# Moving the weighted sums and denominator sums to the end of TensorE's step, and the widening of the maxima behind the step's exponentials

## The chip, the cores and the metric

The kernel runs on one core of a Trainium2 chip. The metric is device time in microseconds (us) of one execution; the times given are medians of several runs. A core has five engines, each of which works through its own list of instructions in the order written: TensorE (matrix products, PE in the profile; its weight loads are PEld), VectorE (DVE), ScalarE (ACT), GpSimd (POOL) and SyncE (SP), which here issues the DMA transfers. [...]

## The reference, cut to what matters

The input is 8 sequences of 1024 rows of 512 numbers. Three stages follow each other, each added to its input:

```
x = x + 0.5 * ffn(layernorm(x))
x = x + attention(layernorm(x))
x = x + 0.5 * ffn(layernorm(x))

ffn(l):        q_l = round(l / scale of the row), q_r = round(rhs / scale of the column), both int8
               (q_l @ q_r) * scale of the row * scale of the column
attention(y):  q, k, v = y Wq', y Wk', y Wv'      16 heads of 32
               q, k = layernorm within each head, with gain and offset
               att = softmax(causal(q k' / sqrt(512)))
               (att v) Wo' + bo
```

What the change concerns is the attention: for each head, the scores, the exponentials of the scores less a maximum per row, their sums weighted by v, and the sums of the exponentials (the denominators).

## The kernel before, in words

**Units.** A unit is one sequence and one group of four heads: 8 x 4 = 32 units (`units`, class `Unit`). Each unit goes through a projection of its rows to q, k and v (`project`, `take`, `squares`, `logs`, `divide`, `turn`), a first pass over the scores to get each row's maximum (`m_*`), and a second pass for the exponentials and sums (`e_*`). The three are done in three successive iterations k: while unit k does its second pass, unit k+1 does its first pass and unit k+2 is projected. The feed-forward stages are cut into blocks of 128 rows (`First` before the attention, `Last` after it) and spread over the same iterations.

**Steps.** An iteration has 20 steps. Nothing is left to a scheduler: every piece of work is entered in a table by `at(k, s, rank, function)`, for iteration k, step s (which may exceed 19 and then falls into the next iteration) and a rank. The last loop of the kernel walks the steps in order, and in a step the entries by rank, and calls them. Each call writes its instructions at the end of the lists of the engines that it uses. So the rank is the order within a step on every engine's list at once, DMA issues on SP included. Ranks are named in one line:

```
    FILL, SUM, MISC, REST, BULK, ADD = range(6)
```

**FILL** (`fill`, L709) is the core of a step: causal masks for the first pass (`m_masks`, L480: bfloat16 matmuls with full 128 x 128 weights), the score matmuls of first and second pass in turn (L496, L566: weights of 32 rows, so that four heads share the array), then VectorE's maximum (`m_max`, L514, L523) and ScalarE's exponential (`e_exp`, L589). Where a block touches the diagonal, GpSimd zeroes the masked half of the exponentials (L593). The last unit has no first pass and does its steps in pairs (`fill_both`).

**SUM** holds `e_sum` (L621), the weighted sums: float32 matmuls with weights of 128 rows and 32 columns, one block of columns for each of the four heads, so a third form of the array. `e_sum(i)` is due two steps after the first half of the exponentials that it reads, at step 2i+2: every even step from 2 to 20. It also holds `e_den` (L639), the sums of the denominators, with weights of ones in the same form, at steps 10 and 22, and ScalarE's copy of the result (L647), which `e_fold` at the next step sends off by four DMAs. `e_den` reads what `e_add` (L609, GpSimd; in the last unit also VectorE) has added up from all blocks.

**MISC** holds transposes and the products of the feed-forward: `flip` (L299, at even steps; it transposes the rounded input that ScalarE wrote at L294 and copies the result at L301), `product` (L306), `spread` (L348), `turn` (L456), and `m_both` (L530), in which VectorE merges two sets of maxima at step 17. **REST** holds work of the other engines: `take`, `e_out`, `e_fold`, loads and stores. **BULK** holds the large matmuls with full weights: `Unit.project` (L402, half a block of rows in each step) and `Last.project` (L368, L370). **ADD** holds `e_add`, and at the end of the first pass `m_wide`, `m_turn` and `m_shift`: ScalarE widens the 32 maxima of a partition to 1024 numbers (L535), TensorE transposes them (L543), VectorE adds them to q (L553), so that the second pass's scores come out less the maximum.

**Buffers.** Each of the accumulators of scores, `p_s` and `p_t`, has one buffer, so the scores of a step wait for the maximum and the exponential of the step before. `ps_x` is one buffer in turn for `flip`, `product`, `spread`, `turn` and `e_den`. Exponentials have four buffers of each of two kinds.

Of the kernel before, what the change touches and what calls it, by code (L numbers as in the profile page):

```python
# [55 lines left out]
def macaron_kernel(  # L56
# [198 lines left out]
    def places(pool, **bufs):  # L255
        return {tag: (pool, tag, n) for tag, n in bufs.items()}
# [482 lines left out]
    def at(k, s, rank, fn, *args):  # L739
        plan[k * STEPS + s].append((rank, len(plan[k * STEPS + s]), fn, args))  # L740

    bufs = places(work, y=3, qn=2, qT=2, f=3, xin=2, x1r=1, x2=1)
    FILL, SUM, MISC, REST, BULK, ADD = range(6)
    def last(f, k, s0):
        at(k, s0, BULK, f.project, 0)
        at(k, s0 + 1, BULK, f.project, 1)
        for s, rank, fn in (
            (-1, REST, f.load),
            (2, REST, f.begin),
            (3, REST, f.root),  # L750
            (4, REST, f.scale),
            (5, REST, f.whole),
            (6, MISC, f.flip),
            (7, MISC, f.product),
            (8, REST, f.add),
            (9, REST, f.store),
        ):
            at(k, s0 + s, rank, fn)

    for k in range(-1, NU + 1):  # L760
        eu = units[k] if 0 <= k < NU else None
        mu = units[k + 1] if 0 <= k + 1 < NU else None
        pu = units[k + 2] if 0 <= k + 2 < NU else None
        for s in range(STEPS):
            m = mu if s < 2 * len(MTILES) else None
            if k == NU - 1:
                if s % 2 == 0:
                    at(k, s, FILL, fill_both, eu, s // 2)
            elif eu is not None or m is not None:
                at(k, s, FILL, fill, eu, m, s)  # L770
        if eu is not None:
            for i in range(len(ETILES)):
                at(k, 2 * i + 2, SUM, eu.e_sum, i)
                for pr in range(2):
                    eng = nc.vector if k == NU - 1 and pr else nc.gpsimd
                    at(k, 2 * i + pr + 1, ADD, eu.e_add, i, pr, eng)
            for hf, s in ((0, 7), (1, 21)):
                at(k, s, REST, eu.e_out, hf)
            for hf, s in ((0, 7 if k == NU - 1 else 10), (1, 22)):
                at(k, s, SUM, eu.e_den, hf)  # L780
                at(k, s + 1, REST, eu.e_fold, hf)
                at(k, s + 3, REST, eu.e_rec, hf)
                at(k, s + 5, REST, eu.e_wide, hf)
                at(k, (15 if k == NU - 1 else 20, 31)[hf], REST, eu.e_mult, hf)
        if mu is not None:
            at(k, 17, MISC, mu.m_both)
            at(k, 17, ADD, mu.m_wide)
            at(k, 18, ADD, mu.m_turn)
            at(k, 18, ADD, mu.m_shift, 0)
            at(k, 18, ADD, mu.m_shift, 1)  # L790
        if pu is not None:
            for t in range(NT):
                s = 2 * t if t < 4 else 2 * t + 2
                at(k, s, BULK, pu.project, t, 0)
                at(k, s + 1, BULK, pu.project, t, 1)
                at(k, s + 2, REST, pu.take, t)
            for j, s in enumerate((4, 8, 14, 18)):
                at(k, s + 1, REST, pu.squares, j)
                at(k, s + 2, REST, pu.logs, j)
                at(k, s + 3, REST, pu.divide, j)  # L800
            for j, s in enumerate((11, 13, 21, 23)):
                at(k, s, MISC, pu.turn, j)

        b, j = divmod(k + 6, 4)
        if 0 < b < B and (b, j) != (1, 0):
            for n in range(2):
                f = First(b, 2 * j + n, ps_x, bufs)
                for s, rank, fn in (
                    (2, REST, f.load),
                    (4, REST, f.begin),  # L810
                    (5, REST, f.root),
                    (6, REST, f.scale),
                    (7, REST, f.whole),
                    (8, MISC, f.flip),
                    (9, MISC, f.product),
                    (10, REST, f.add),
                    (11, REST, f.store),
                    (12, REST, f.root2),
                    (13, REST, f.norm2),
                    (16, MISC, f.spread),  # L820
                ):
                    at(k, s + 10 * n, rank, fn)

        b, j = divmod(k, 4)
        b -= 1
        if 0 <= b < B - 1:
            for n in range(2):
                last(Last(b, 2 * j + n, ps_x, bufs), k, (10 * n + 8) if k < NU - 1 else (6 * n + 4))
# [49 lines left out]
```

## Time and profile before

| what | value |
|---|---|
| median of 3 runs | 2504.11 us (2503.69 to 2505.66) |
| profiled execution, its own time | 2508.39 us |
| its span, first to last instruction | 2506.7 us |
| TensorE, VectorE, GpSimd, ScalarE busy | 95%, 71%, 67%, 49% of the span |
| mean granted TensorE clock | 0.988 |
| score matmuls busy, first pass L496, second pass L566 | 656.6 and 663.2 us |
| q, k, v projections busy, L402 | 773.7 us |
| weighted sums busy, L621 | 340.7 us |
| additions of exponentials busy on GpSimd, L609 | 1109.7 us |
| widening of the maxima, L535, 32 times | 1.06 us each |

From about 170 us to about 2320 us the iterations follow one another with little difference, some 67 us each; before that lies the preparation of weights and the first sequence, after it the last unit and the last blocks of the output. A busy time of TensorE is a sum over modelled ends of overlapping matmuls, so a lost tenth of a microsecond is more safely read from the starts of successive groups than from idle time.

### The profile page before, as it was taken

What the parts mean: (1) busy time and instruction counts of PE and PEld (TensorE: products, weight loads), DVE (VectorE), ACT (ScalarE), POOL (GpSimd) and SP (SyncE); (2) the same over time, 40 slices, a digit from 0 to 9 for tenths busy, and PEclk for the clock granted to TensorE, in tenths of its full rate; (3) what the DMA queues carried; (4) which work ended last, traced back from release to release, by engine and by line L of the source; (5) the groups of instructions that cost most, each with busy time, mean ns of one, the idle gap of its engine ahead of it and who ended that gap; (6) DMA issues with size and microseconds to landing.
All of it is one profiled execution on the core that took longest, in us unless ns stands there. A gap on an engine that the chain in (4) does not pass through costs nothing.

```text
span 2506.7 us, 40820 instructions
## 1 busy us (share of the span) xinstructions
PE 2392.0 (95%) x15448; PEld 1099.6 (44%) x15448; DVE 1778.8 (71%) x3053; ACT 1237.1 (49%) x2409; POOL 1681.9 (67%) x1790
## 2 busy tenths in 40 slices
PE   3999999999999999999999999999999999999785
PEld 1544444444444444444444444444444444444332
DVE  9566777777777777777777777777777776666664
ACT  2335555555554555555555555555555555545441
POOL 3227777776777776677777667777767776666672
PEclk9899999999999999999999999999999999999997
DMA  4000000111110111111011111111111100000011
GB/s 143 30 18 22 27 26 27 31 41 38 33 42 31 43 35 35 39 35 43 31 43 35 35 39 35 43 32 35 44 35 39 35 28 25 27 27 27 26 43 59
DMA packets 79303, 92.86 MB, mean 37 GB/s; under 512 B 30977, under 2 KB 37121, under 8 KB 79106
## 3 DMA queue, kind: packets, MB, share of 16 engines
q1 hardware_dynamic: 79106, 90.26, 11.8%
q8 instruction: 121, 1.98, 0.3%
q14 instruction: 76, 0.62, 0.1%
HBM read 55.60 MB, written 34.08 MB: 36 GB/s over the span
## 4 chain that ended last, share of the span: by engine, by line
PE 76%; DVE 12%; POOL 7%; issue 4%; SPq 1%; ACT 1%; DMA 1%; DVEq 0%; POOLq 0%; ACTq 0%
PE p_qkv L402 22%; PE p_s L496 17%; PE p_o L621 9%; PE p_w_b L370 8%; PE p_t L566 6%; POOL pt L609 4%; DVE nm L523 3%; PE p_f_b L306 2%; PE p_d L639 2%; PE p_s L480 2%; PE p_f_a L306 2%; PE p_h L456 2%; POOL f_b L313 2%; DVE oT L674 1%; PE p_m L543 1%
## 5 line engine op out<-in xcount | busy, mean ns | idle before, releaser
L609 POOL TENSOR_TENSOR pt<-pt,pt 128x768 f32<-128x768 f32 (+1 forms) x630 | 1109.7, 1764 | 127.0 <-ACT pt L589 108.5
L589 ACT ACTIVATE pt<-p_t 128x1024 f32<-128x1024 f32 (+1 forms) x640 | 599.4, 938 | 982.4 <-PE p_t L566 908.4
L523 DVE TENSOR_REDUCE nm<-p_s 128x2 f32<-128x1024 f32 (+2 forms) x640 | 632.9, 1006 | 525.8 <-PE p_t L566 409.6
L402 PE MATMUL p_qkv<-wall,yT_a 128*128 128x384 f32 x2048 | 773.7, 501 | 0.2 <-ACT v L421 0.2
L496 PE MATMUL p_s<-qk 32*128 32x512 f32 (+3 forms) x3072 | 656.6, 524 | 14.1 <-DVE nm L523 12.4
L566 PE MATMUL p_t<-qk 32*128 32x512 f32 (+3 forms) x3072 | 663.2, 526 | 2.0 <-ACT pt L589 2.0
L402 PEld LDWEIGHTS p_qkv<-wall,yT_a 128*128 128x128 f32 x2048 | 354.7, 191 | 287.3 <-issue 136.6
L593 POOL TENSOR_SCALAR_AFFINE_SELECT pt<-pt 128x256 f32<-128x256 f32 x512 | 227.6, 457 | 215.6 <-ACT pt L589 214.2
L621 PE MATMUL p_o<-pt,v 128*32 128x512 f32 (+3 forms) x3072 | 340.7, 497 | 11.8 <-POOL pt L593 11.6
L496 PEld LDWEIGHTS p_s<-qk 32*128 32x128 f32 x3072 | 227.5, 185 | 198.0 <-DVE nm L523 65.6
L566 PEld LDWEIGHTS p_t<-qk 32*128 32x128 f32 x3072 | 238.7, 183 | 52.2 <-ACT pt L589 23.5
L370 PE MATMUL p_w_b<-wo,oT 128*128 128x512 f32 x512 | 244.3, 600 | 0.0
L621 PEld LDWEIGHTS p_o<-pt,v 128*32 128x32 f32 x3072 | 75.1, 108 | 247.8 <-issue 159.0
L313 POOL TENSOR_TENSOR f_a<-f_a,xin_a 128x512 f32<-128x512 f32 x64 | 90.9, 1420 | 84.2 <-DVE f_a L310 84.2
L480 PEld LDWEIGHTS <-ident_bf 128*128 128x128 bf16 x1024 | 83.5, 98 | 135.9 <-issue 81.2
L462 ACT ACTIVATE qk<-p_h,qk_b,qk_g 128x256 f32<-128x256 f32 x256 | 130.1, 563 | 11.9 <-PE p_h L456 11.9
L370 PEld LDWEIGHTS p_w_b<-wo,oT 128*128 128x128 f32 x512 | 97.6, 192 | 78.0 <-issue 69.1
L480 PE MATMUL p_s<-causal_bf,ident_bf 128*128 128x128 bf16 x1024 | 110.2, 220 | 8.6 <-DVE nm L523 5.8
L514 DVE TENSOR_REDUCE nm<-p_s 128x4 f32<-128x1024 f32 x64 | 77.6, 1212 | 47.2 <-PE p_t L566 42.6
L417 ACT ACTIVATE sq<-p_qkv 128x256 f32<-128x256 f32 x256 | 99.1, 387 | 21.7 <-PE p_qkv L402 15.1
L420 ACT COPY c<-p_qkv 128x256 f32<-128x256 f32 x256 | 96.8, 378 | 4.3 <-PE p_h L456 4.3
L313 POOL TENSOR_TENSOR f_b<-f_b,x_b 128x512 f32<-128x512 f32 x64 | 89.9, 1405 | 8.9 <-DVE f_b L310 8.9
(108 smaller groups left out, 2474.0 us busy)
## 6 DMA issues: line engine op xcount, KB each, us to landing
xin_a<-in_x_dram SPq DMA_DIRECT2D x64, 256.0 KB, 2.8
x1d_a<-f_a SPq DMA_DIRECT2D x64, 256.0 KB, 2.2
rb<-rdr SPq DMA_DIRECT2D x256, 64.0 KB, 2.0
x1r_b<-x1d_a SPq DMA_DIRECT2D x64, 256.0 KB, 2.9
out_dram<-f_b SPq DMA_DIRECT2D x64, 256.0 KB, 2.1
dsq<-dsb SPq DMA_DIRECT2D x256, 2.0 KB, 1.7
rT<-in_rhsT_dram SPq DMA_DIRECT2D x4, 256.0 KB, 3.6
wall<-in_wqT_dram SPq DMA_DIRECT2D x4, 256.0 KB, 5.8
```

The lines of the kernel that those rows point to most:

```text
L313: nc.gpsimd.tensor_tensor(self.f, self.f, self.src, ALU.add)
L370: nc.tensor.matmul(self.p_w, oT[self.b, g, hf][:, o : o + P], wo[:, g, :], start=False, stop=(g == NG - 1),)
L402: nc.tensor.matmul(self.p[:, : 3 * P], yT[self.b, t][:, kc, :], wall[:, kc, self.g].rearrange("p a f -> p (a f)"), start=(kc == 0), stop=( ...
L462: nc.scalar.activation(self.qk[:, a, 2 * j * P : (2 * j + 2) * P], p_h[:, a].rearrange("p t i -> p (t i)"), AF.Identity, scale=qk_g[:, a : ...
L480: nc.tensor.matmul(self.pm[:, hh, c0 + n - P : c0 + n], ident_bf, causal_bf, start=not self.pm_begun, stop=False, skip_group_check=True,)
L496: nc.tensor.matmul(self.pm[:, hh, c0 : c0 + n], self.rows(0, h, it * P, P), self.rows(1, h, ch * HALF, n), start=not self.pm_begun and sub ...
L523: nc.vector.tensor_reduce(self.nm[:, ch, it, hs], self.pm[:, :, c0 : c0 + n], AX.X, ALU.max, negate=True)
L566: nc.tensor.matmul(self.pes[pr][:, hh, c0 : c0 + n], self.rows(1, h, jt * P, P), self.rows(0, h, hf * HALF + o, n), start=True, stop=True, ...
L589: nc.scalar.activation(pt[:, :, :cols], self.pes[pr][:, :, :cols], AF.Exp, scale=scale)
L593: nc.gpsimd.affine_select(out=pt[:, :, c0 : c0 + P], in_=pt[:, :, c0 : c0 + P], compare_op=ALU.is_ge, fill=0.0, base=0, pattern=[[0, 2], [ ...
L609: eng.tensor_tensor(acc[:, :, o : o + n], acc[:, :, o : o + n], pt[:, :, c0 : c0 + n], ALU.add)
L621: nc.tensor.matmul(self.p_o[h * HD : (h + 1) * HD, o : o + n], self.v[:, jt, h * HD : (h + 1) * HD], self.pt[i, h // 2][:, h % 2, c0 : c0 ...
```

## The change

Two edits in the table of steps; no instruction is added or removed. The rank SUM goes from second place to fifth: within a step, `e_sum` and `e_den` now come behind MISC, REST and BULK, and ahead of ADD only. And `m_wide` goes from the end of step 17 (rank ADD) to step 18 at rank MISC, where it stands right behind that step's FILL, ahead of `flip`'s and `take`'s copies on ScalarE; `m_turn`, which needs it, stays at the end of step 18.

```
-    FILL, SUM, MISC, REST, BULK, ADD = range(6)
+    FILL, MISC, REST, BULK, SUM, ADD = range(6)
...
         if mu is not None:
             at(k, 17, MISC, mu.m_both)
-            at(k, 17, ADD, mu.m_wide)
+            at(k, 18, MISC, mu.m_wide)
             at(k, 18, ADD, mu.m_turn)
             at(k, 18, ADD, mu.m_shift, 0)
             at(k, 18, ADD, mu.m_shift, 1)
```

More of the change, by code (lines that the diff above doesn't have):

```diff
@@ L742, in macaron_kernel @@
     bufs = places(work, y=3, qn=2, qT=2, f=3, xin=2, x1r=1, x2=1)
-    FILL, SUM, MISC, REST, BULK, ADD = range(6)
+    FILL, MISC, REST, BULK, SUM, ADD = range(6)
     def last(f, k, s0):
@@ L786, in macaron_kernel @@
             at(k, 17, MISC, mu.m_both)
-            at(k, 17, ADD, mu.m_wide)
+            at(k, 18, MISC, mu.m_wide)
             at(k, 18, ADD, mu.m_turn)
```

## The prediction

> **What bounds the kernel now.** I read the busy row first, then TensorE's waits between 180 and 2320 us (before lie the weights, after it the last unit), then TensorE's instructions in order of time in one unit, then those of GpSimd and ScalarE in the same microseconds.
>
> ```profile
> PE 2392.0 (95%) x15448; PEld 1099.6 (44%) x15448; DVE 1778.8 (71%) x3053; ACT 1237.1 (49%) x2409; POOL 1681.9 (67%) x1790
> ```
>
> TensorE sets the time. Its waits:
>
> ```profile
> PE p_o L621 <- POOL pt L593: 10.3, 26, 0.7
> PE p_s L496 <- DVE nm L523: 6.6, 26, 0.6
> ```
>
> That looks like 10 us to win. But idle time counts from a modelled end, so I measure from start to start. TensorE, steps 18 and 19 of unit 16 (columns: start, length, then the group):
>
> ```profile
> 1224.94 0.70 PE L566 MATMUL p_t<-qk 32*128 32x256 f32 x4
> 1225.57 0.84 PE L621 MATMUL p_o<-pt,v 128*32 128x384 f32 x4
> 1226.77 1.06 PE L621 MATMUL p_o<-pt,v 128*32 128x384 f32 x12 [0.36 <-POOL pt L593]
> 1227.76 0.40 PE L299 MATMUL p_t_a<-ident_bf,qn_a 128*128 128x128 bf16 x4
> 1228.00 0.38 PE L368 MATMUL p_w_b<-bo,ones_bf 128*128 128x512 bf16 x1
> 1228.21 1.88 PE L370 MATMUL p_w_b<-wo,oT 128*128 128x512 f32 x4
> 1229.93 1.04 PE L543 MATMUL p_m<-ident,nmw 128*128 128x128 f32 x8
> ```
>
> The weighted sum `e_sum(8)` takes 1227.76 - 1225.57 = 2.19 us. The same sixteen matmuls unwaited:
>
> ```profile
> 2335.59 1.07 PE L621 MATMUL p_o<-pt,v 128*32 128x384 f32 x16
> 2336.59 0.40 PE L299 MATMUL p_t_b<-ident_bf,qn_b 128*128 128x128 bf16 x4
> ```
>
> 1.00 us, so 1.19 is lost where the wait says 0.36. Who is late? GpSimd, then ScalarE:
>
> ```profile
> 1222.47 1.55 POOL L313 TENSOR_TENSOR f_b<-f_b,x_b 128x512 f32<-128x512 f32 x1
> 1223.98 2.35 POOL L609 TENSOR_TENSOR pt<-pt,pt 128x1024 f32<-128x1024 f32 x1
> 1226.28 0.80 POOL L593 TENSOR_SCALAR_AFFINE_SELECT pt<-pt 128x256 f32<-128x256 f32 x2
> ```
>
> ```profile
> 1224.62 0.62 ACT L294 ACTIVATE qn_a<-y_a 128x512 bf16<-128x512 f32 x1
> 1226.40 1.06 ACT L535 ACTIVATE nmw<-nm 128x1024 f32<-128x1024 f32 x1 [1.15 <-DVE nm L530]
> 1227.36 0.58 ACT L589 ACTIVATE pt<-p_t 128x512 f32<-128x512 f32 x1
> ```
>
> The masking (L593) of step 17's exponentials stands behind an addition of the feed-forward and one of denominators. ScalarE has waited 1.15 us for the maxima, and step 18's exponential stands behind that; nobody on TensorE waits for it.
>
> **What the Trainium skill says.** TensorEngine Tiling (Array Packing), Key Properties: a change of tiling mode drains TensorE. The trace agrees: 384-column matmuls with full weights start 0.322 us apart, but 0.414 pass from the last to the first score matmul (1203.803 to 1204.217), so 0.09 is the drain. Perfetto Trace Analysis, Tensor Engine Instruction: the end of a matmul is estimated, not observed; 0.36 against 1.19 shows what that hides. SBUF — State Buffer, SBUF: two separate sides: VectorE with two inputs in SBUF and GpSimd lock each other out. L530 is 0.18 us at its shortest and 1.55 at the median, and here ends at 1226.36, with the addition on GpSimd (1226.33). That is why the maxima are late.
>
> **Part 1, sums to the end: what it removes.** I compared each run of matmuls of one kind with the shortest of the same shapes and neighbours. Between 200 and 2310 us only these exceed it noticeably.
> - `e_sum(8)`, step 18: 1.17 us in units 4 to 25, 0.59 in units 0 to 3, 0.27 in 26 to 29, 1.16 in 30. In front of it now come the transposes `flip` (0.23) and `Last.project` (1228.00 to 1229.93, plus a drain: 2.03). That is more than the 1.19 needed; in units 0 to 3 only `flip` is there, and 0.33 of 0.59 is won. 22 x 1.17 + 4 x 0.33 + 4 x 0.27 + 1.16 = 29.3 us.
> - `e_sum(9)`, step 20, units 0 to 3: 1.29 each. A projection (1.49) comes in front: 5.2 us.
> - Scores waiting for VectorE's maxima at steps 13 and 14: 0.14 + 0.27 in 22 units, 8.9 us. The same work lies between the same scores, so I count nothing; they are the upside.
> Removed: 34.5 us.
>
> **What it adds.** Modes in order before: scores (32x128), sum (128x32), full weights, next scores: three changes. After: scores, full, sum, scores: three again. But where the next step opens with the causal masks, which have full weights, they followed the full matmuls without a change, and now follow the sum.
>
> ```profile
> 1220.88 1.46 PE L402 MATMUL p_qkv<-wall,yT_a 128*128 128x384 f32 x4
> 1222.17 0.28 PE L480 MATMUL p_s<-causal_bf,ident_bf 128*128 128x128 bf16 x2
> 1222.37 0.70 PE L496 MATMUL p_s<-qk 32*128 32x512 f32 x2
> ```
>
> 1.29 us for the projection into masks, where into scores it takes 1.385 (the median of those behind a transpose): one drain more. The change from full weights to a sum appears once without a wait:
>
> ```profile
> 2433.35 0.39 PE L368 MATMUL p_w_b<-bo,ones_bf 128*128 128x512 bf16 x1
> 2433.58 1.88 PE L370 MATMUL p_w_b<-wo,oT 128*128 128x512 f32 x4
> 2435.39 0.64 PE L621 MATMUL p_o<-pt,v 128*32 128x256 f32 x8
> ```
>
> 2.04 us against 1.94 (2316.42 to 2318.36) into more full weights: 0.093 to the nanosecond. Four masks behind a sum take 0.327 (2331.37 to 2331.70), behind full weights 0.316. So about 0.10 each. Masks open odd steps 1, 3, 5, 9, 17, all behind a sum: 31 units x 5, less six with nothing moved in between, 149 x 0.10 = 14.9 us. In step 18 the transposes `m_turn` (0.97 us, 1229.93 to 1230.90) followed full weights and now follow the sum: a drain of 0.093 plus weights that load uncovered, 0.057 by the first float32 transpose after a change (0.165, later ones 0.109): 31 x 0.15 = 4.7 us. I take 0.10 and 0.15; the ends are 0.08 to 0.15 and 0.13 to 0.25, that is 16 to 30 us together.
>
> **Other things moved, costed at nothing.** `flip` loses its cover: it now follows the scores. Its input was done 0.27 to 0.59 us before the sum began (here 1225.24 against 1225.57), so no wait; the margin is thin in 102 flips. `spread`'s input has over 5 us, buffers of the projections 2.7 and more. `e_den` ends a step: its copy L647 (0.59) is ready 1.28 us after the last matmuls' start (tail: 2441.30 to 2442.58), and `turn` wants the bank after 0.54 + 1.07 = 1.61. Queued behind the copy on ScalarE is the next exponential, which needs later scores anyhow. SP's four `e_fold` DMAs come about 1.5 us later; behind them stand the store of `x1d`, the next loads and the reciprocal's DMA, due two steps (7 us) on. GpSimd's `e_add(4)` waits for `e_sum(3)`, some 2 us later; it sat idle 3.0 us before and 3.1 after (start 1190.9).
>
> **Part 2, the widening.** L535 (1.06) starts behind step 18's exponential, which moves from 1227.36 to about 1225.7; L535 itself stays near 1226.4, held by L530, and ends 1227.5. `m_turn` needs it near 1228.8. Behind it stand `flip`'s copy (to 1228.1) and three of `take` (1.06), wanted in steps 19 and 20. Gain and loss: nothing; uncovered it would cost up to 1 us in 31 units.
>
> **Last unit.** Steps have no projections to move past, but a `flip` at step 10 that waits for ScalarE (0.34) now waits in front of the sum (+1.1), and some eight changes of mode (0.8 in all); `flip` at step 22 no longer waits for `e_den`'s copy (-1.7), yet that sum comes 2.4 us later, with over 3 to spare before its reciprocal at 2450.24 (DMAs issued until 2444.96, 1.7 to land). I take +2, between -2 and +4.
>
> **Sum.** -34.5 + 14.9 + 4.7 + 2 = -12.9 us. The profiled execution took 2508.4 us (span 2506.7), so 2495.5; the median 2504.1 stands 4.3 below it and gives 2491.2. Ends: -34.5 + 16 - 2 = -20.5 (2483.6) and -34.5 + 30 + 4 = -0.5 (2503.6).
>
> **Rivals.**
> - The listed wait is the true one: 10.3 us plus little, less 20 and 2: +11, 2515. Against it, start to start shows 1.19. Chance 0.04.
> - GpSimd stays late: as TensorE arrives sooner, half the wait comes back at `e_sum(9)` or in the next unit: -17 + 22 = +5, 2509. Against it, GpSimd idles 2 to 3 us at several places in each unit. 0.12.
> - Slower: `flip` waits. Its margin is a median 0.33 to 0.59. If its input comes later by the margin plus d, TensorE loses 102 x d; from d = 0.17 the result is over 2509, at 0.25 it is 2517. For it: the thin margin. Against: nothing ahead of L294 on ScalarE or VectorE moves. 0.08.
> - The upside: VectorE's 8.9 us go too: 2482. For it, masks at step 9 start 0.1 later; against, the lag begins at step 11. 0.10.
> - My sum, 0.66, mostly 2484 to 2504.
>
> A measurement can't tell 0.2% (5.0 us) from no change. Below 2499.1: most of my sum (0.6), the upside, little else: 0.72. Within: 0.16. Above 2509.1: 0.12. To hold eight in ten I take 2481 to 2507.
>
> **What would show it.** Step 18: score, flip, project, then one group of sixteen L621 of 1.0 us without a wait, `m_turn` of about 1.03 right behind. Odd masked steps longer by 0.10. The wait L621 for L593 near zero. Wrong if waits appear at L299 for L294, or if changes of mode cost over 0.19 each (34.5 / 180).

## The result, and the profile after

The changed kernel takes 2493.72 us (median of 5 runs, 2492.61 to 2494.24) against 2504.11 us before; the ratio is 0.9961 with a 95% interval of 0.9946 to 0.9975, so between 6 and 14 us faster. Predicted were 2491.2 us and -12.9 us. The profiled execution took 2492.61 us with a span of 2490.9; the one of before had 2506.7, and was itself some 4 us slower than its median.

The first part of the page hardly changes: TensorE is as full as it was.

```profile
PE 2377.0 (95%) x15326; PEld 1082.3 (43%) x15448; DVE 1780.6 (71%) x3053; ACT 1222.0 (49%) x2409; POOL 1678.6 (67%) x1790
```

Some 122 matmul records are missing from this trace, so that of the sums is taken from starts, not from busy time. TensorE's waits between 180 and 2310 us:

```profile
PE p_s L496 <- DVE nm L523: 6.6, 26, 0.6
PE p_w_b L370 <- issue: 1.3, 8, 0.2
PE p_m L543 <- ACT nmw L535: 0.9, 4, 0.2
PE p_s L480 <- DVE nm L523: 0.9, 1, 0.9
```

The wait of the weighted sums L621 for the masking L593 is gone (10.3 us before); that of the scores for VectorE's maxima is the same to a tenth; a new one, of 0.9 us in all, is that of `m_turn` for the widened maxima. The second line stands where the record of the matmul in front (L368) is among those missing. TensorE in step 18 of unit 16, the step shown of before:

```profile
1214.46 0.70 PE L566 MATMUL p_t<-qk 32*128 32x256 f32 x4
1215.09 0.40 PE L299 MATMUL p_t_a<-ident_bf,qn_a 128*128 128x128 bf16 x4
1215.54 1.88 PE L370 MATMUL p_w_b<-wo,oT 128*128 128x512 f32 x4
1217.35 1.07 PE L621 MATMUL p_o<-pt,v 128*32 128x384 f32 x16
1218.35 1.09 PE L543 MATMUL p_m<-ident,nmw 128*128 128x128 f32 x8
1219.38 0.70 PE L566 MATMUL p_t<-qk 32*128 32x256 f32 x4
```

The sum is one group of sixteen and takes 1.00 us (1217.35 to 1218.35) where it took 2.19. The transposes behind it take 1.03 us (1218.35 to 1219.38) where they took 0.97. From the first score of step 18 to the first of step 19 pass 4.92 us; before it was 5.96. GpSimd and ScalarE in the same stretch:

```profile
1213.37 2.35 POOL L609 TENSOR_TENSOR pt<-pt,pt 128x1024 f32<-128x1024 f32 x1
1215.67 0.79 POOL L593 TENSOR_SCALAR_AFFINE_SELECT pt<-pt 128x256 f32<-128x256 f32 x2
```

```profile
1215.27 0.60 ACT L589 ACTIVATE pt<-p_t 128x512 f32<-128x512 f32 x1 [0.51 <-PE p_t L566]
1215.78 1.05 ACT L535 ACTIVATE nmw<-nm 128x1024 f32<-128x1024 f32 x1
```

GpSimd is nearly as late: its masking ends at 1216.46, 1.37 us after TensorE went on from the scores of step 18 (1215.09); before it was 1.51 (1227.08 against 1225.57). Only, TensorE now has other work until 1217.35. ScalarE no longer sits idle for the maxima.

What did it cost? Step 16 ends like this, with the masks of step 17 behind the sum:

```profile
1209.29 1.46 PE L402 MATMUL p_qkv<-wall,yT_a 128*128 128x384 f32 x4
1210.68 1.07 PE L621 MATMUL p_o<-pt,v 128*32 128x512 f32 x8
1211.68 0.28 PE L480 MATMUL p_s<-causal_bf,ident_bf 128*128 128x128 bf16 x2
1211.89 0.70 PE L496 MATMUL p_s<-qk 32*128 32x512 f32 x2
```

The projection takes 1.39 us into the sum, where it took 1.29 into the masks. I read that 0.09 to 0.10 us as the added change of the array's mode; e3 and e9 below test it.

A unit's length is best measured from one unit's first `m_turn` (L543) to the next one's, in the instructions in order of time. The table gives it for the units with the same make-up, worked out so from each profile. It also shows that units differ more than the "some 67 us each" given for the kernel before: from 66 to 74 us.

| kernel | units 1 to 3 | units 5 to 25 | units 27 to 29 | first L543 to last, us |
|---|---|---|---|---|
| before | 66.02 | 73.57 | 69.49 | 2223.5 |
| the change | 65.03 | 73.08 | 69.91 | 2208.7 |
| e1, sums alone | 65.06 | 73.09 | 69.91 | 2206.4 |
| e2, widening alone | 66.02 | 73.57 | 69.49 | 2223.3 |
| e3, sums of steps 2, 4, 8, 16 | 66.22 | 73.88 | 69.80 | 2230.6 |
| e4, sum of step 18 (20 in 0 to 3) | 64.84 | 72.41 | 69.22 | 2188.5 |
| e9, e4 with `m_turn` behind | 64.83 | 72.55 | 69.37 | 2191.5 |

So the change is a gain of 0.49 us in each of 21 units and of 0.99 in three, and a loss of 0.42 in three. Of the 15.8 us between the two spans, 14.8 lie between the first and the last L543. The 2.0 us ahead of it touch nothing that was changed; that stretch varies between 158.5 and 161.6 us over all but one of the profiles of this study. The last stretch is 1.0 us longer.

### The profile page after: what moved, and what is told of

It is laid out like the page before. It is cut to its first block, busy times and chain, and to the rows that moved or that the text cites. A ratio compares the mean times of both kernels' runs of the same rounds, so it can differ in the third digit from the quotient of the medians.

```text
span 2490.9 us, 40698 instructions
## 1 busy us (share of the span) xinstructions
PE 2377.0 (95%) x15326; PEld 1082.3 (43%) x15448; DVE 1780.6 (71%) x3053; ACT 1222.0 (49%) x2409; POOL 1678.6 (67%) x1790
## 4 chain that ended last, share of the span: by engine, by line
PE 83%; DVE 12%; issue 3%; ACT 1%; SPq 1%; POOL 1%; DMA 0%; DVEq 0%; POOLq 0%; ACTq 0%
PE p_qkv L402 24%; PE p_s L496 18%; PE p_o L621 10%; PE p_w_b L370 9%; PE p_t L566 7%; DVE nm L523 3%; PE p_s L480 3%; PE p_d L639 2%; PE p_f_b L306 2%; PE p_h L456 2%; PE p_f_a L306 2%; PE p_y_a L348 1%; PE p_m L543 1%; DVE oT L674 1%; DVE amax_b L281 1%
## 5 line engine op out<-in xcount | busy, mean ns | idle before, releaser
L593 POOL TENSOR_SCALAR_AFFINE_SELECT pt<-pt 128x256 f32<-128x256 f32 x512 | 226.0, 453 | 199.3 <-ACT pt L589 194.1
L621 PE MATMUL p_o<-pt,v 128*32 128x512 f32 (+3 forms) x3072 | 315.8, 496 | 0.0
L621 PEld LDWEIGHTS p_o<-pt,v 128*32 128x32 f32 x3072 | 72.2, 109 | 209.0 <-issue 160.2
L480 PEld LDWEIGHTS <-ident_bf 128*128 128x128 bf16 x1024 | 71.5, 98 | 171.4 <-issue 134.4
```

The source lines that it names most:

```text
L480: nc.tensor.matmul(self.pm[:, hh, c0 + n - P : c0 + n], ident_bf, causal_bf, start=not self.pm_begun, stop=False, skip_group_check=True,)
L593: nc.gpsimd.affine_select(out=pt[:, :, c0 : c0 + P], in_=pt[:, :, c0 : c0 + P], compare_op=ALU.is_ge, fill=0.0, base=0, pattern=[[0, 2], [ ...
L621: nc.tensor.matmul(self.p_o[h * HD : (h + 1) * HD, o : o + n], self.v[:, jt, h * HD : (h + 1) * HD], self.pt[i, h // 2][:, h % 2, c0 : c0 ...
```

## The experiments

All are timed in turn with the kernel before on the same chip; its medians there were 2505.7 to 2507.4 us, so each is read by its ratio.

**The two halves apart (e1, e2).** e1 is the change without this edit, e2 is this edit alone:

```
-            at(k, 17, ADD, mu.m_wide)
+            at(k, 18, MISC, mu.m_wide)
```

> Theory (all of the gain comes from the sums' new rank): about -10 us, the same as the whole change, 2493 to 2495; m_turn still finds its input, since the widening was held by VectorE's merge of the maxima in both places. Rival (the widening's place matters, because step 18's exponential no longer stands behind it): at least 3 us of the gain are missing here, and units 0 to 3 wait at step 20 again.

> Theory (nothing on TensorE waited for the exponential behind the widening): no change, 2502 to 2506. Rival (the exponential of step 18 comes 1.6 us earlier and GpSimd's masking with it): 3 us or more faster.

e1 took 2494.39 us (ratio 0.9958, 0.9945 to 0.997), e2 2505.82 us (1.0003, 0.9995 to 1.0011). The order of the sums carries everything. The widening's place is worth nothing, in either order of the sums: units of 5 to 25 differ by 0.01 us. In units 1 to 3 of the change it moves time from one step to the next: `m_turn` waits for it, and step 18 takes 3.42 us where e1 has 3.14, but step 19 takes 1.80 where e1 has 2.10.

**Where the order only costs (e3).** The sums go to the end in four steps in which they had not waited, and with them the sum of the denominators that falls into step 2.

```
+    FILL, SUM, MISC, REST, BULK, TURN, LATE, ADD = range(8)
+    late = k < NU - 1 and i in (0, 1, 3, 7)
+    at(k, 2 * i + 2, LATE if late else SUM, eu.e_sum, i)
+    at(k, s, LATE if k < NU - 1 and hf else SUM, eu.e_den, hf)
```

> The sums go to the end only in steps 2, 4, 8 and 16 of iterations 0 to 30, where the next step opens with masks and no sum waited. Theory (each such sum adds one change of the array's mode, 0.10 us): 122 x 0.10 = +12 us, about 2516. Rival (a change of mode is hidden, or the order within a step is free): 2504 within 2 us.

It took 2513.49 us, 1.0033 (1.0021 to 1.0046): slower by 5 to 12 us where I expected 12. A unit grows by 0.31 us and not by 4 x 0.10. The trace shows why: the sum of step 18, measured from its first start to the next group's, takes 2.04 to 2.08 us here and 2.16 to 2.20 before (iterations 4 to 25). In one unit:

```profile
1230.87 0.84 PE L621 MATMUL p_o<-pt,v 128*32 128x384 f32 x4
1231.92 1.06 PE L621 MATMUL p_o<-pt,v 128*32 128x384 f32 x12 [0.22 <-POOL pt L593]
1232.91 0.40 PE L299 MATMUL p_t_a<-ident_bf,qn_a 128*128 128x128 bf16 x4
```

The tenth that step 16 loses is taken from the wait of step 18, since GpSimd's masking does not come later with it. The three other steps show it in full: 0.093 us for the projection's end into the sum, and 0.01 for the masks behind the sum (0.327 against 0.316 for four). In the change itself, where step 18 no longer waits, nothing absorbs the fourth.

**Only where the sum waits (e4).** In step 18 the transposes of the maxima also come ahead of the sum, from iteration 4 on, so that they keep their neighbours of the same mode (LATE and TURN are the ranks of e3).

```
+    late = k < NU - 1 and (i == 8 or i == 9 and k < 4)
+    at(k, 2 * i + 2, LATE if late else SUM, eu.e_sum, i)
+    at(k, 18, MISC, mu.m_wide)
+    at(k, 18, TURN if k >= 4 else ADD, mu.m_turn)
```

> The sum goes to the end only in step 18, and in step 20 of iterations 0 to 3; in step 18 the transposes of the maxima come ahead of it from iteration 4 on, so that they follow full weights. Theory (only there did the sum wait, and without the masked steps nearly no change of mode is added): -34.5 + 1 = -33 us, 2469 to 2474, faster than both kernels. Rival (as TensorE comes sooner, GpSimd is late elsewhere): half of it, 2485 or more, with waits of L621 for L593 at another step.

It took 2473.32 us, 0.9875 (0.986 to 0.989), and again 2473.13 (0.9869, 0.9853 to 0.9886). That is some 32 us faster than before and some 20 faster than the change. Its TensorE, one unit:

```profile
1207.50 0.40 PE L299 MATMUL p_t_a<-ident_bf,qn_a 128*128 128x128 bf16 x4
1207.95 1.88 PE L370 MATMUL p_w_b<-wo,oT 128*128 128x512 f32 x4
1209.67 1.04 PE L543 MATMUL p_m<-ident,nmw 128*128 128x128 f32 x8
1210.64 1.07 PE L621 MATMUL p_o<-pt,v 128*32 128x384 f32 x16
1211.64 0.70 PE L566 MATMUL p_t<-qk 32*128 32x256 f32 x4
```

The projection takes 1.72 us into the transposes, and these 0.97 into the sum. A unit is 1.16 us shorter than before: the whole wait of 1.17. The change has 0.67 us more in a unit than this kernel: five masked steps and the transposes, for which the prediction had 5 x 0.10 + 0.15 = 0.65.

**The price of the transposes' place (e9).** e4 without its last line.

> The kernel with only step 18's sum moved, but with the transposes of the maxima left behind the sum, as in the change. Theory (full weights to sum to full weights is one change of mode more, 0.093, and the first transpose's weights load uncovered, 0.06): the unit is 0.15 us longer than with the transposes ahead, 27 units x 0.15 = +4 us, about 2477.5. Rival (the price is in the masked steps alone): no difference, 2473.

> The same kernel as e4_step18, beside e9_turn_behind on the same chip, so that the two are compared there: 2470 to 2476.

2473.46 us (2471.85 to 2475.68) beside 2473.13 (2470.37 to 2474.98): the medians do not tell them apart. The profiles do: a unit is 72.55 us against 72.41, 0.14 where 0.15 was expected, and the difference lies in step 18 (4.92 us against 4.77). But the stretch behind the last L543 is 4.0 us shorter than in the second profile of e4 (120.8 against 124.8), which hides it in the total. The granted clock differs there: 0.91 in that stretch of e9, 0.88 in that of e4. I take the price as shown by the units, and its share of the time as not measured.

**Was GpSimd's order the cause? (e5)** The sums stay early; one addition goes behind the masking that it held up.

```
-    at(k, 2 * i + pr + 1, ADD, eu.e_add, i, pr, eng)
+    late = k < NU - 1 and (i, pr) == (7, 1)
+    at(k, 2 * i + pr + 1 + late, ADD, eu.e_add, i, pr, eng)
```

> The sums stay early; on GpSimd alone one addition of denominators (block 7, second pair of heads) goes from the end of step 16 to the end of step 17, behind the masking of step 17's exponentials. Theory (the sum of step 18 waits because that masking stands behind this addition): the wait of step 18 goes, about -27 us, 2476 to 2481; a little may come back at step 20. Rival (GpSimd is late by its whole load, not by the order): the wait moves to step 20 in all units, gain under 12 us.

It took 2491.15 us, 0.9937 (0.9923 to 0.9951): -16 us, not -27. In units 5 to 25 the reading holds: they shrink to 72.48 us, by 1.09. Step 18 gains 1.16, and step 20 loses 0.07. But units 1 to 3 grow from 66.0 to 68.2, and 27 to 29 from 69.5 to 70.3. In units 27 to 29 the sum of step 20 waits 1.06 us. Units 1 to 3 gain 0.59 in step 18 and lose 2.03 in step 19 by a new wait of TensorE, the first line below. What is late there stands in the rows after it, of GpSimd and VectorE around one step 18:

```profile
PE p_s L480 <- DVE qk L553: 9.0, 4, 2.3
```

```profile
290.31 5.48 POOL L609 TENSOR_TENSOR pt<-pt,pt 128x1024 f32<-128x1024 f32 x3
290.40 2.32 DVE L445 TENSOR_TENSOR hh<-hh,hss 128x16 f32<-128x16 f32 x1
```

Three additions now follow one another, and an operation of VectorE on 16 columns, 0.18 us at its median and 1.76 at most in the kernel before, takes 2.32. It ends with the first addition (292.71 and 292.68); the next one, L447, takes 1.73 and ends with the second. The shift of q stands behind them, and the next unit's masks wait for that. A further 0.7 to 0.8 us goes in step 20 of these units. Behind the new wait the granted clock was 0.50 for 3.4 us (from 229.2 and 297.5 us on, and twice more), while the kernel before had 1.00 throughout these units; whether the clock or GpSimd costs these 0.7 us no run tells. So the delay in step 18 belongs to GpSimd's order, and a new order puts it somewhere else unless the steps there have room.

**What flip lost (e6, e7).** ScalarE writes the input of each flip (L294) three times instead of once, in the changed kernel (e6) and in the one before (e7); the added writes repeat the first.

```
+            nc.scalar.activation(self.qn, self.y, AF.Copy, bias=-ROUND)
+            nc.scalar.activation(self.qn, self.y, AF.Copy, bias=-ROUND)
```

> Sums at the end, and ScalarE writes the rounded input of each transpose (L294) three times instead of once, so that it is ready some 1.1 us later. Theory (the sum no longer covers flip; its margin is 0.27 to 0.59 us): 102 waits of 0.5 to 0.8 us, +50 to +75 us over the changed kernel, 2545 to 2570. Rival (flip has cover from elsewhere): under +15 us.

> The same three writes with the sums early. Theory (the sum of 1.0 us stands between the scores and flip, margin 1.38 to 2.5 us): hardly any wait, 2503 to 2512, and the masking or the exponentials behind it are not late enough to matter. Rival (the added 110 us of ScalarE delay the exponentials): over 2520 here too.

e6 took 2612.05 us (1.042, 1.0405 to 1.0434), by the ratios some 115 us more than the change, where I expected 50 to 75; e7 2519.23 (1.0051, 1.0037 to 1.0066), 12 more than before and outside the 2503 to 2512 that I expected. TensorE's waits of e6 between 180 and 2310 us (the two added lines move L299 to L301 and L294 to L296):

```profile
PE p_t_a L301 <- ACT qn_a L296: 44.2, 52, 1.0
PE p_t_b L301 <- ACT qn_b L296: 41.4, 48, 1.0
```

A unit of 5 to 25 grows by 3.68 us: 0.78, 1.05, 0.84 and 1.00 in its four flips, from the last matmul's start to flip's. In e7 the same units are 73.59 us long, as before. Its loss lies behind the last L543, a stretch of 137.8 us where before it was 122.7; there TensorE waits 30.3 us for L294's result in nine flips (18.4 before). The margin is thus what I read off, and it is all that is left. My figure for e6 was too small for two reasons. I took 1.1 us for two writes; they start 0.66 us apart, so 1.32. And I left out the stretch behind the last L543, which is 22 us longer in e6 than in the change; 95 us more lie between the first L543 and the last.

**The upside (e8).** The scores of steps 13 and 14 wait for VectorE. In e4 I took the product with the reciprocals out of step 11:

```
-    at(k, (15 if k == NU - 1 else 20, 31)[hf], REST, eu.e_mult, hf)
+    at(k, (15 if k == NU - 1 else 20, 31 if k == NU - 1 else 30)[hf], REST, eu.e_mult, hf)
```

> The kernel with only step 18's sum moved, and VectorE's product of the second half (e_mult, L674) goes from step 31 to step 30, that is from step 11 to step 10 of the next iteration. Theory (the scores of steps 13 and 14 wait for maxima because this product of 1.03 us stands in front of them on VectorE, which idles 1.6 us in front of step 11's maximum): the 0.14 + 0.27 us of 22 units go, -9 us, about 2464. Rival (the wait comes from VectorE's whole load, or the product waits for its DMA and blocks the maxima earlier): no gain or slower.

It took 2488.75 us, 0.9927 (0.9915 to 0.9939): by the ratios 13 to 15 us more than e4, where I expected 9 less. GpSimd and VectorE in step 11, and the wait of step 13:

```profile
1194.16 2.34 POOL L609 TENSOR_TENSOR pt<-pt,pt 128x1024 f32<-128x1024 f32 x1
...
1194.75 1.79 DVE L442 TENSOR_SCALAR hss<-hss 128x16 f32<-128x16 f32 x1
...
1199.75 0.70 PE L496 MATMUL p_s<-qk 32*128 32x512 f32 x2 [0.74 <-DVE nm L523]
```

L442 takes 0.16 us in e4, where the product stood in front of it and the addition on GpSimd was over when it began. Here it begins inside the addition and ends with it (1196.54 and 1196.50). VectorE gains 1.03 us and loses 1.63, and the wait of step 13 becomes 0.8 by the starts instead of 0.14. The cause of the waits of steps 13 and 14 stays open between the amount of VectorE's work and the additions on GpSimd under which its operations take longer; this run shows only that moving the product is no cure.

## Why the prediction was right

- **The removed wait, -34.5 us.** Right in size, and in place from iteration 4 on. The 22 waits of 1.17 us went in full (e4: 1.16 per unit). Units 27 to 29 were to change by -0.27 + 0.65 = +0.38; measured +0.42. Units 1 to 3 were to change by -0.33 - 1.29 + 0.65 = -0.97; measured -0.99, but by other parts. Step 20 loses its 1.29 as forecast. Step 18 gains nothing, not 0.18, because the transposes wait for the widening; step 19 is 0.11 shorter; and the change of mode added in step 8 costs nothing there, since the masks behind it wait for VectorE's maximum in both kernels (they start 0.06 us after it ends, and the step takes 2.91 us). That these came to the forecast total is luck.
- **Idle time against starts.** The rival that took the listed 10.3 us as the true loss is out: e4 gains about 32 us. But the modelled ends are the smaller part of what that list hides. In the sum shown of before, the single matmuls start in twos (1225.570 and 1225.576, then 1225.916 and 1225.923, then from 1226.774 on); in the unwaited one they start in fours, within 0.02 us (2335.589 to 2335.609). Two heads run first, the two with the late masking after them, each pair for the time in which all four could have run. From the starts I estimate 0.51 us of standing still (1225.916 + 0.34 to 1226.774), of which 0.36 is listed, and 0.68 us of running two at a time. The 1.19 us stand; the prediction put the whole difference to 0.36 down to modelled ends.
- **The added changes of mode, +19.6 us.** 0.65 per unit expected, 0.67 measured. The drain taken from one place in the last unit (0.093) came out again: in the step 18 shown, `Last.project` takes 1.81 us into the sum and took 1.72 into the transposes, and so, to 0.002 us, at all 52 places between 200 and 2310 us where it goes into a sum.
- **GpSimd comes late elsewhere.** Not in the change: no wait of a sum is listed any more, at any step. By the starts, only the sum of step 18 in iterations 0 to 3 still loses time, 0.15 us (e1: 1.156 us from its start to the transposes, where unwaited sums take 1.00); the prediction had left 0.26. In e5, which reorders GpSimd itself, this rival's mechanism does appear.
- **flip waits.** Not in the change: the times from the end of L294 to flip were 0.28 to 0.59 us between 200 and 2310 us, once 0.10, and no wait is listed there. e6 shows that the danger was real.
- **VectorE's 8.9 us.** Unchanged, as counted.
- **The widening, nothing.** Right for the time (e1, e2). In step 18 of iterations 0 to 3 it was not hidden, as said above.
- **Last unit, +2.** +1.0 in the profile behind the last L543, which is less than this stretch varies from profile to profile (120.8 to 126.2 us, e6 and e7 aside). `flip` at step 10 did wait 1.34 us in front of the sum, 1.0 more than before.
- **The sum.** Between the first and the last L543 it was to be -34.5 + 19.6 = -14.9 us, and the two profiles differ by 14.8. That this is right to a tenth is luck too: the last unit-to-unit interval in it differs by 1.5 us between the two profiles, and runs from 61.4 us (e9, granted clock 0.97 there) to 65.6 (before, 0.92). The medians differ by 10.4. The profiled execution of before took longer than its median, at a granted clock of 0.988. Of its 17 runs beside e1, the two at 0.991 took 2499.0 and 2500.6 us, those at 0.989 2503.1 to 2506.8, and the one at 0.987 2507.9, so the clock may be what parts the two differences; I could not settle which is nearer. The prediction lies within the measured interval.

## What to carry to other kernels

When a matrix engine is full, compare each group's time from start to start with the shortest group of the same shape: here that found three times what the table of waits listed, in the sum taken apart above mainly because matmuls that could run side by side ran one after the other. Moving work that waits behind work that doesn't is worth it exactly where it waits; done everywhere, it paid back 20 of 33 us in changes of the array's mode, so move the one step and keep operations of one mode together. Before moving, measure how long ago the moved-up work's input was ready, for that margin is all that is left.

## What the runs showed of the hardware

In these kernels a change between full weights, weights of 32 rows and weights of 32 columns costs 0.09 to 0.12 us from start to start. Into a sum or scores it is 0.093: a half of `project` behind a transpose takes 1.386 us into either and 1.293 into masks. Out of a sum it is 0.11 to 0.12: eight matmuls of 512 columns take 0.882 us into more of their form, 0.996 into `project` and 0.998 into masks. The first group of the new form also takes longer: 0.10 us for a half of `project` (1.394 us into masks behind scores, 1.293 behind a transpose), 0.06 for the transposes of the maxima (1.022 against 0.966), 0.01 for the masks. I read this as weights that load uncovered; no run shows it. That each of these is even, to a few nanoseconds from 200 to 2300 us, I had not expected. Nor that a VectorE operation on 16 columns can take 2.32 us when it starts under an addition on GpSimd, so that taking work away in front of it makes it later.
